# Masked attention: the row of maxima is transposed and spread two slots later, behind the fourth block of scores

## The chip, the core and the metric

The kernel runs on one core of a Trainium2 chip. The metric is the device time of one launch in microseconds (us); the time given is the median over runs. TensorE is called PE here, VectorE DVE, ScalarE ACT, GpSimd POOL, and SyncE, which issues the DMAs, SP.

## The reference, cut to what matters

Four layers, each added to its input: a masked attention, a modulated attention, and two recurrences over 256 steps. The change is in the first one. Its input x is 8 batches of 256 x 512 in float32; queries, keys and values are one and the same projection:

```python
q = xt @ Wq.T
qh = q.reshape(B, T, NH, dk).transpose(0, 2, 1, 3)      # 8 heads of 32
scores = scale * jnp.einsum('bhqd,bhkd->bhqk', qh, qh)
logits = (scores * cmask + (1.0 - cmask) * NEG) * rmask
attn = jax.nn.softmax(logits, axis=-1)
ctx = jnp.einsum('bhqk,bhkd->bhqd', attn, qh)
out = ctx @ Wo.T                                        # x = x + transposed out
```

Softmax is a quotient of sums of exponentials, so any number that is taken off all scores of one query cancels; it only keeps the exponentials in range. The kernel takes the query's largest score.

## The kernel before

Both attentions run interleaved in one loop over slots, `for g in range(-5, ...)`, U = 8 slots to a batch of the masked attention. A batch has two halves e of four heads each, and each half has four blocks kc of 128 keys. Within a slot the program is written out by hand: every engine gets its instructions in the order of the calls in the loop's body. `at(g, rel, n)` says which batch and which step r stand at slot g: it takes g - rel as 8 b + r.

A half passes through these steps:

- `scores0` (L205), slot 8b - 4 + 4e + kc: PE makes the scores of one block for four heads in four PSUM banks (s, L211), ACT copies them to a tile sc of 128 x 2048 (L216).
- `maxima0` (L219), same slot: DVE reduces sc to one maximum for each head and each row of the block, into a column of mxp0[e] (L221). The scores are symmetric, so rows of keys are as good as rows of queries. In the slots of blocks 0 to 2 it is called in the middle of the slot, in that of block 3 near its end.
- `rows0` (L225), once for each half: PE turns mxp0[e] into rows (pm, four transposes, L229), ACT copies them to mrow (L231), SP writes four rows, 8 KB, to DRAM (row, L234), and, when that has landed, reads them back for all 128 partitions (bc, 1 MB, L235). mrow and bc have one buffer each. So a new bc has to wait until the last block of the half before has used the old one.
- `weights0` (L237), slot 8b + 1 + 4e + kc: DVE takes bc off sc (L239). `exps0` (L241): ACT makes the exponentials (L243).
- `values0` (L245), slot 8b + 2 + 4e + kc: PE sums values and exponentials (pc, L254). `weigh0` (L262), after the fourth block: DVE's reciprocals (r, L271) and products, POOL's mask (ctxT, L273 and L274).
- `masked_out` (L276): the output projection (pso, L281), added to x by DVE (L284).

Before, rows0 stands at `at(g, -5, U)` with r = 3 or 7, that is in slots 8b - 2 and 8b + 2: in the slot of the third block of scores. At that place in the slot, the maxima of blocks 0 and 1 of this half have been called for; the columns of blocks 2 and 3 still hold what an earlier batch left there. Only the very first half (slot -1) has its rows made behind its own fourth block, by a call of its own.

The second attention fills the same slots: `qkv` (psqkv, L321), `maxima1` (n, L372, and its reduction L380), `rows1` (L382, with a copy mrow1 on ACT, L387), `weights1` (L389 to L411), `values1` (pc, L167), `modulated_out` (psx, L425). Its turned result is stored for later by `modulated_turn` (x2d, L448) on the same SP queue as row and bc, and so are the loads of x and mask for a batch to come (L78, L80). All score tiles, transposes and projections of both share one pool of five PSUM banks, handed out in turn. In slots whose number is 4 to 7 modulo 8, from 20 on, a1 is set (up to slot 63), and scores0 and rows0 are called behind the second attention's maxima1 and values1.

Of the kernel before, what the change touches and what calls it, by code (L numbers as in the profile page):

```python
# [24 lines left out]
def attention(ctx, tc, cst, x, cond, wqT, woT, w_emb, b_emb, g_norm, w_qkv, g_q, g_k, w_out, follow):  # L25
# [21 lines left out]
    U = 8  # L47
# [157 lines left out]
    def scores0(b, e, kc):  # L205

        qm = qms[b]
        ss = [bank([P, D], f"s0_{b}_{e}_{kc}_{h}") for h in range(4)]
        for h in range(4):
            r = 32 * h  # L210
            nc.tensor.matmul(  # L211
                ss[h], lhsT=qm[r : r + 32, e, kc * P : (kc + 1) * P], rhs=qm[r : r + 32, e, :], start=True, stop=True
            )
        sc = ftwo.tile([P, 4, D], F32, tag="sc", name=f"sc_{b}_{e}_{kc}", bufs=7)
        for h in range(4):
            nc.scalar.copy(sc[:, h, :], ss[h])  # L216
        scs[b, e, kc] = sc
# [7 lines left out]
    def rows0(b, e):  # L225

        pt = bank([P, NJ, P], f"pm0_{b}_{e}")
        for qc in range(NJ):
            nc.tensor.transpose(pt[:, qc, :], mxp0[e][:, qc, :], ident)  # L229
        mrow = ftwo.tile([P, D], F32, tag="mrow", name=f"mrow0_{b}_{e}", bufs=1)  # L230
        nc.scalar.copy(mrow, pt.rearrange("p q n -> p (q n)"))  # L231
        bc = bcs[b, e] = ftwo.tile([P, 4, D], F32, tag="bc", name=f"bc_{b}_{e}", bufs=1)
        row = dram.tile([4, D], F32, tag="row", name=f"row_{b}_{e}", bufs=2)
        nc.sync.dma_start(row, mrow.rearrange("(h i) n -> h i n", i=32)[:, 0, :])  # L234
        nc.sync.dma_start(bc, row.rearrange("h n -> (h n)").partition_broadcast(P).rearrange("p (h n) -> p h n", h=4))  # L235

    def weights0(b, e, kc):  # L237
        sc = scs[b, e, kc]
        nc.vector.tensor_sub(sc, sc, bcs[b, e])  # L239
# [22 lines left out]
    def weigh0(b, e):  # L262

        fill = ftwo.tile([P, D], F32, tag="fill", name=f"fill_{b}_{e}", bufs=1)
        nc.gpsimd.tensor_scalar(fill, mks[b], -1.0, means[b, e], ALU.add, ALU.mult)
        cx = ctxTs[b][:, e, :]
        pv, pn = pc0s[b, e]
        for i in range(2):
            t = slice(256 * i, 256 * i + 256)
            r = sm.tile([P, 256], F32, tag="r", name=f"r_0_{b}_{e}_{i}", bufs=2)  # L270
            nc.vector.reciprocal(r, pn[:, t])  # L271
            nc.vector.scalar_tensor_tensor(cx[:, t], r, 1e30, pv[:, t], ALU.min, ALU.mult)
        nc.gpsimd.tensor_tensor(cx, cx, mks[b], ALU.mult)  # L273
        nc.gpsimd.tensor_tensor(cx, cx, fill, ALU.add)  # L274
# [87 lines left out]
    def maxima1(b, c):  # L362
        qT, kT = qTs[b], kTs[b]

        ss = []
        for h in range(4):
            n = f"n1_{b}_{c}_{h}"
            ss.append(other_bank([P, 2, 256], f"c{h}", n) if b == B - 1 and h < 2 else bank([P, 2, 256], n))
        for qc in range(2):
            for h in range(4):  # L370
                r = 32 * h
                nc.tensor.matmul(  # L372
                    ss[h][:, qc, :],
                    lhsT=qT[r : r + 32, c, qc * P : (qc + 1) * P],
                    rhs=kT[r : r + 32, c, :],
                    start=True,
                    stop=True,
                )
        for h in range(4):
            nc.vector.tensor_reduce(mxp1[:, :, 32 * h], ss[h], AX.X, ALU.max)  # L380
# [32 lines left out]
    def values1(b, c):  # L413
        if c == 0:
            oTs[b] = big.tile([P, NJ, 256], F32, tag="oT", name=f"oT_{b}")
        pc = other_bank([P, 2, 256], "c2", f"pc1_{b}_{c}")
        for half in range(2):
            values(pc, half, lambda k, h: vts[b][:, k, c * P + h * DH : c * P + (h + 1) * DH], [exs1[b, c]])
        weigh(pc, oTs[b][:, c, :], f"1_{b}_{c}")
# [44 lines left out]
    def at(g, rel, n=1):  # L464

        b, r = divmod(g - rel, U)
        return (b, r) if 0 <= b < B and r < n else None

    def heads(g, rel, which=range(B)):

        for b in which:
            if 0 <= g - HEADS[b] - rel < NJ:
                return b, g - HEADS[b] - rel
        return None
# [3 lines left out]
    def leave(kind):  # L478
        for key in [k for k in left if k[0] == kind]:
            yield *key[1:], left.pop(key)  # L480

    with tc.manual_schedule():
        for g in range(-5, OUT[-1][1] + 2):

            a0, v0 = at(g, -4, U), at(g, 2, U)
            w1, v1 = heads(g, 1), heads(g, 2)

            a1, early = heads(g, 1, range(B - 2)), heads(g, 0, range(B - 2, B))
            late = a1 is not None or heads(g, 0, range(B - 2)) is not None
            turns = list(leave("qkv"))  # L490
            if a1:
                maxima1(*a1)
                if v1:
                    values1(*v1)
                if a := due.pop("weigh", None):
                    weigh0(*a)
            elif a0:
                scores0(a0[0], a0[1] // 4, a0[1] % 4)
            if (a := at(g, -5, U)) and a[1] % 4 == 3 and g > 0 and not a1:
                rows0(a[0], a[1] // 4)  # L500
            if v0 and not late:
                values0(v0[0], v0[1] // 4, v0[1] % 4)
            for a in leave("qt"):
                project_out(*a)
            if g == OUT[-1][1] + 1:
                cst["soon"]()
            for a in leave("x2"):
                modulated_turn(*a)
            if g - 1 in norms:
                modulate(norms.index(g - 1))  # L510
            if a1 and a0:
                scores0(a0[0], a0[1] // 4, a0[1] % 4)
            if (a := at(g, -5, U)) and a[1] % 4 == 3 and a1:
                rows0(a[0], a[1] // 4)
            if w1:
                rows1(*w1)
            if e0 := at(g, 1, U):
                weights0(e0[0], e0[1] // 4, e0[1] % 4)
                if not late:
                    exps0(e0[0], e0[1] // 4, e0[1] % 4)  # L520
            if v0 and not late and v0[1] % 4 == 3:
                weigh0(v0[0], v0[1] // 4)
            if a0 and a0[1] % 4 < 3:
                maxima0(a0[0], a0[1] // 4, a0[1] % 4)

            if a := at(g, -5, 2):
                left["qt", a[0], a[1]] = project(*a)
            if a := at(g, U + 2):
                masked_out(a[0])
            if 3 <= g < 7:  # L530
                modulation(2 * g - 6)
            if g == U:
                add_identity()
            if g in norms:
                normalize(norms.index(g))
            made = [(part, qkv(*part)) for part in parts.get(g, ())]
            for b in range(B):
                if g in OUT[b]:
                    m = OUT[b].index(g)
                    left["x2", b, m] = modulated_out(b, m)  # L540
            if a0 and a0[1] % 4 == 3:
                maxima0(a0[0], a0[1] // 4, 3)
            if g == -1:
                rows0(0, 0)
            for part, lines in made:
                if lines:
                    qkv_norm(*part, *lines)
                    left["qkv", *part] = lines[1]
            if not w1:
                for a in turns:  # L550
                    qkv_out(*a)
            if early:
                maxima1(*early)

            if v1 and not a1:
                values1(*v1)
            if w1:
                weights1(*w1)
                for a in turns:
                    qkv_out(*a)  # L560
            if e0 and late:
                exps0(e0[0], e0[1] // 4, e0[1] % 4)
            if v0 and late:
                values0(v0[0], v0[1] // 4, v0[1] % 4)
                if v0[1] % 4 == 3:
                    due["weigh"] = v0[0], v0[1] // 4
            if (a2 := at(g, -7)) and a2[0] > 1:
                load(a2[0])
            if g == -1:
                load_weights()  # L570
            if g == U * B + 2:
                first.close()
                follow()
                for (b, m), d in x2d.items():
                    nc.sync.dma_start(
                        cst["x2T"][:, :, b, m * P : (m + 1) * P], d.rearrange("p (j n) -> p j n", j=NJ)
                    )
# [486 lines left out]
```

## Time and profile before

| what | us |
|---|---|
| median of 3 runs | 2914.75 |
| lowest and highest | 2910.18, 2915.89 |
| the profiled execution, whole | 2913.32 |
| its span in the trace | 2910.6 |
| the two attentions, start to about | 836 |
| DVE: subtraction of bc (L239), one | 2.28 |
| DVE: maxima of a block (L221), one | 2.28 |
| ACT: copy to mrow (L231), one | 0.63 |
| PE: one transpose of maxima (L229) | 0.27 |

The span is the time between the first and the last instruction of one execution, and the rest of the execution lies around it. The chain that ended last is followed back from the last instruction: at each step to what released it, or to the instruction before it on its engine. "Waits" lists who stood idle for whom. In the chain and in waits, a name like `pm` is the tile that is written, with the number of the batch left out; `L229` is the line in the code above. PEld is PE's load of the stationary operand, which overlaps its matmuls. PEclk is the granted clock of PE, as a share of full speed.

### The profile page before, as it was taken

To read this page: it belongs to the slowest core of one execution; us is meant where nothing else is said; L and a number is where in the kernel's file an instruction comes from. 1 tells how busy PE (TensorE), PEld (TensorE's weight loads), DVE (VectorE), ACT (ScalarE), POOL (GpSimd) and SP (SyncE) were. 2 spreads that over 40 slices of the span, in tenths; PEclk is the share of its full clock that TensorE was granted. 3 is DMA by queue.
4 is the path that set the end of the run, shared out by engine and by line. 5 is a ranking of instruction groups with operands and counts; after the bars stand their busy time and mean duration, and the time that the engine had idled before them with its cause. 6 is when DMAs were issued, how large, how long until landed. Compare 5 with 4: busy or idle time off the path is not lost.

```text
span 2910.6 us, 159805 instructions
## 1 busy us (share of the span) xinstructions
PE 2705.6 (93%) x67258; PEld 1918.5 (66%) x67258; DVE 2126.1 (73%) x8951; ACT 1718.5 (59%) x8427; POOL 1098.7 (38%) x2945
## 2 busy tenths in 40 slices
PE   7799999999989999999999999999999999999996
PEld 3234444444557777777777777777777777777775
DVE  6767777676357777777777777777777777777774
ACT  5666566654346666666666666666666666666552
POOL 1144333443213444444444344444444434444442
PEclk8899999999999999999999999999999999999999
DMA  3111010101600000000000000000000000000000
GB/s 146 40 41 48 27 45 27 48 16 37 131 2 5 6 7 7 6 7 7 7 6 6 7 6 6 7 6 6 7 7 6 6 7 7 6 7 6 7 6 7
DMA packets 27558, 57.58 MB, mean 20 GB/s; under 512 B 2816, under 2 KB 17164, under 8 KB 24788
## 3 DMA queue, kind: packets, MB, share of 16 engines
q1 hardware_dynamic: 26836, 47.36, 5.5%
q8 instruction: 525, 8.60, 1.2%
q14 instruction: 197, 1.61, 0.2%
HBM read 40.15 MB, written 7.21 MB: 16 GB/s over the span
## 4 chain that ended last, share of the span: by engine, by line
PE 57%; DVE 29%; ACT 8%; issue 4%; POOL 1%; DMA 1%; ACTq 0%; SPq 0%; POOLq 0%; DVEq 0%
PE pg L795 19%; PE ic L760 18%; DVE icT L952 5%; PE psqkv L321 5%; DVE qn L953 5%; ACT tT L660 4%; DVE hqs L913 3%; PE pc L254 3%; DVE own L810 3%; DVE sqmm L909 2%; DVE v L812 2%; PE pc L167 2%; DVE hz L840 2%; PE s L211 2%; PE n L372 1%
## 5 line engine op out<-in xcount | busy, mean ns | idle before, releaser
L760 PE MATMUL ic<-cT_sb,tT 128*8 128x128 f32 x32736 | 1087.3, 273 | 82.4 <-ACT tT L660 44.6
L760 PEld LDWEIGHTS ic<-cT_sb,tT 128*8 128x8 f32 x32736 | 761.5, 89 | 340.1 <-ACT tT L660 271.6
L795 PE MATMUL pg<-whh_sb,hz 128*32 128x128 f32 x24576 | 819.0, 274 | 49.8 <-DVE hz L840 16.8
L660 ACT ACTIVATE tT<-qn 128x16 f32<-128x16 f32 x2046 | 439.8, 216 | 641.8 <-DVE qn L953 514.2
L795 PEld LDWEIGHTS pg<-whh_sb,hz 128*32 128x32 f32 x24576 | 667.8, 110 | 124.4 <-DVE hz L840 123.9
L952 DVE STREAM_TRANSPOSE icT<-ic 128x64 f32<-128x64 f32 x2048 | 504.2, 246 | 69.7 <-PE ic L760 64.7
L953 DVE SCALAR_TENSOR_TENSOR qn<-icT,hqs 128x16 f32<-128x16 f32 x2048 | 350.7, 171 | 70.1
L755 POOL TENSOR_TENSOR W<-W,cx 128x128 f32<-128x128 f32 x765 | 297.3, 389 | 256.1 <-ACT cx L741 256.0
L748 POOL TENSOR_TENSOR W<-cx,us 128x128 f32<-128x128 f32 x255 | 116.9, 458 | 446.4 <-ACT cx L741 446.4
L909 DVE SCALAR_TENSOR_TENSOR sqmm<-sqmm,qn 128x32 f32<-128x32 f32 x768 | 153.5, 200 | 151.5 <-ACT sqmm L898 122.9
L913 DVE TENSOR_TENSOR hqs<-W,sqmm 128x32 f32<-128x32 f32 x1020 | 199.9, 196 | 46.5 <-DVE own L835 1.1
L774 PE MATMUL gi<-wih_sb,x3T 128*32 128x384 f32 (+2 forms) x3072 | 202.4, 379 | 0.5 <-POOL x3T L965 0.5
L741 ACT ACTIVATE cx<-qn 128x32 f32<-128x32 f32 x1280 | 200.9, 213 | 0.2
L321 PE MATMUL psqkv<-wqkv_sb,xnT 128*128 128x512 f32 x384 | 174.6, 600 | 2.2 <-ACT sc L216 1.7
L221 DVE TENSOR_REDUCE mxp<-sc 128x4 f32<-128x2048 f32 x64 | 145.9, 2282 | 39.9 <-ACT sc L216 39.9
L741 ACT ACTIVATE cx<-p 128x32 f32<-128x32 f32 x1020 | 149.8, 217 | 32.3 <-DVE p L908 1.6
L216 ACT COPY sc<-s 128x512 f32<-128x512 f32 x256 | 131.5, 610 | 49.9 <-PE s L211 49.8
L810 DVE STREAM_TRANSPOSE own<-pg 128x128 f32<-128x128 f32 x256 | 84.8, 331 | 91.8 <-PE pg L795 91.8
L239 DVE TENSOR_TENSOR sc<-sc,bc 128x2048 f32<-128x2048 f32 x64 | 147.4, 2304 | 4.9 <-DMA bc<-row 4.8
L741 ACT ACTIVATE cx<-q 128x32 f32<-128x32 f32 x1020 | 145.5, 213 | 0.0
L243 ACT ACTIVATE sc<-sc,negT 128x2048 f32<-128x2048 f32 x64 | 129.1, 2019 | 20.2 <-DVE sc L239 20.2
L898 ACT ACTIVATE sqmm<-qn 128x32 f32<-128x32 f32 x768 | 140.4, 183 | 0.4
(149 smaller groups left out, 3353.8 us busy)
## 6 DMA issues: line engine op xcount, KB each, us to landing
bc<-row SPq DMA_DIRECT2D x16, 1024.0 KB
x<-in_x SPq DMA_DIRECT2D x8, 512.0 KB
out<-o SPq DMA_DIRECT2D x256, 16.0 KB
wqkv_sb<-in_L_cond_W_qkv SPq DMA_DIRECT2D x1, 3072.0 KB
wih_sb<-in_L_cond_W_ih SPq DMA_DIRECT2D x4, 768.0 KB
whh_sb<-in_L_cond_W_hh SPq DMA_DIRECT2D x4, 768.0 KB
x2d<-x2o SPq DMA_DIRECT2D x11, 256.0 KB
x2T<-x2d SPq DMA_DIRECT2D x11, 256.0 KB
```

The costliest lines, as they stand in the source:

```text
L321: nc.tensor.matmul(ps, lhsT=xnTs[b][:, c, m * P : (m + 1) * P], rhs=wqkv_sb[:, c, part * D : (part + 1) * D], start=(c == 0), stop=(c == N ...
L660: nc.scalar.activation(tT, src[:, half * HM : (half + 1) * HM, :], AF.Tanh)
L741: nc.scalar.activation(c[:, i], x, AF.Copy, scale=f)
L755: nc.gpsimd.tensor_tensor(W[:, i + 1 : 5], W[:, i + 1 : 5], c, ALU.add)
L760: nc.tensor.matmul(ps[32 * j : 32 * j + B, :], lhsT=tT[k // HM][:, k % HM, :], rhs=cT_sb[:, k, j * P : (j + 1) * P], start=(k == 0), stop= ...
L774: nc.tensor.matmul(gi_ps[rows(j), g0:g1, :], lhsT=x3T[c][:, k, :], rhs=wih_sb[:, k, g0:g1, j * P : (j + 1) * P], start=(k == 0), stop=(k = ...
L795: nc.tensor.matmul(pg_ps[rows(j), :], lhsT=hzs[tau % 3][:, k, 32 * g : 32 * g + 32], rhs=whh_sb[:, k, g, j * P : (j + 1) * P], start=((k, ...
L810: nc.vector.transpose(pgt.rearrange("p m n -> p (m n)"), pg_ps)
L909: stt(mm, sq, LIN[s], qs, ALU.subtract, ALU.mult)
L913: nc.vector.tensor_sub(hq, W[:, s], mm)
L952: nc.vector.transpose(icT.rearrange("p m n -> p (m n)"), ic[:, half * 64 : half * 64 + 64])
L953: stt(qn[:, m2, :], icT[:, :, 0:B], IC[s], hq[:, m2, :], ALU.mult, ALU.add)
```

## The change

rows0 is called two slots later: in slots 8b and 8b + 4, where the first block of the next half has its scores. All four blocks' maxima have been called for by then. Its place within the slot is the same, behind scores0. The half's first subtraction of bc, in slot 8b + 1 + 4e, stays where it was, so one slot lies between the two where there were three. The first half of all (slot -1) is unchanged.

```diff
-            if (a := at(g, -5, U)) and a[1] % 4 == 3 and g > 0 and not a1:
+            if (a := at(g, -3, U)) and a[1] % 4 == 3 and g > 0 and not a1:
                 rows0(a[0], a[1] // 4)
...
-            if (a := at(g, -5, U)) and a[1] % 4 == 3 and a1:
+            if (a := at(g, -3, U)) and a[1] % 4 == 3 and a1:
                 rows0(a[0], a[1] // 4)
```

## The prediction

> **What bounds the kernel now.** I read the page's slices first: TensorE (PE) is 9 tenths busy nearly everywhere, so only the attention stage (0 to about 836 us), which the change touches, can move. Then the chain that ended last, in order of time, because a sum over engines doesn't tell which wait is paid for. "Slot g" is one pass of the loop over g.
>
> Early slots, from the chain (start us, length us, engine, tile, line):
>
> ```profile
> 38.65 0.90 PE pm L229 x3
> 39.56 3.22 PE pc L254 x16
> ...
> 54.35 4.56 DMA bc<-row
> ...
> 67.73 0.90 PE pm L229 x3
> 68.62 3.57 PE pc L254 x16
> 72.20 3.51 PE pe L144 x16
> 75.71 2.06 PE s L211 x8
> ...
> 84.35 5.51 DMA bc<-row
> ...
> 98.67 0.90 PE pm L229 x3
> 99.57 3.57 PE pc L254 x16
> 103.14 3.94 PE pso L281 x8
> ```
>
> Five times before 165 us the chain runs through the transposes of the maxima (pm, L229): slots 2, 6, 10, 14, 18. Slots 2, 6, 10 are above. PE stands there in program order, with all that follows behind it:
>
> ```profile
> PE pm L229 <- DVE mxp L221: 20.3, 7, 9.0
> ```
>
> This is PE's largest wait between 20 and 180 us (us in total, times, longest). And the stretches (busy us per engine, then PEclk) show what a long wait does afterwards:
>
> ```profile
> 58.00:68.00 10.00, 6.17 (x50) 3.40 (x48) 9.00 (x8) 6.59 (x10) 3.16 (x4) 0.91 0.01 4
> 68.00:78.00 10.00, 10.00 (x47) 5.03 (x50) 6.73 (x7) 2.84 (x3) 2.77 (x2) 0.50 0.00 1
> ```
>
> At clock 0.50 the value matmuls (pc, L254) take 3.57 us; at 1.00 they take 1.85 (chain, from 110 us on).
>
> Steady slots (20 to 60, a period of 93.35 us for 8 slots, from row issues at 403.63 and 496.98): the transposes are on the chain in slots 26, 34, 42, 50, 58 alone, without a wait:
>
> ```profile
> 444.67 0.66 PE L229 MATMUL pm<-ident,mxp 128*128 128x128 f32 x4
> ```
>
> In slots 22, 30, 38, ... they aren't. There DVE runs without a gap from 398.07 to 415.5 us, and the chain's next scores wait for its maxima (L380).
>
> **The change part by part.** Counts stay: 15 of the 16 calls of rows0 move two slots later, each with 4 transposes, one copy on ACT (mrow, 0.59 to 0.63 us), a row DMA and a 1 MB bc DMA. DVE's and POOL's own orders are the same. On SP two x2d stores of each middle batch now stand ahead of the second head half's row and bc DMAs instead of behind them: they go out up to 24 us earlier, but between 260 and 700 us no instruction waits for an x2d store, so 0. The load of x behind bc in slots 9, 17, ... is issued as much later as bc is; its buffer is used 7 slots on, so 0.
>
> *1. What the early slots lose.* I follow each engine's order with the trace's own durations.
> Slot 2: pc need not stand behind pm; its exponentials end at 38.49, so it starts near 38.6 instead of 39.5: 0.9 gained.
> Slot 4: pm comes here. The last maxima end near 51.2, PE is free at 50.2: 1.0 wait plus 0.6. Row issue near 52.6, bc at 54.4 (1.75 later, as the chain has it for the first row), so the first subtraction (L239) of slot 5 is at 58.96 against 58.93: gain back to 0.
> Slot 6: pm would have waited 3.17 us behind maxima that stand behind two reciprocals on DVE. Without it pc starts at 64.7, not 68.6, and warm: 1.85 + 1.85 for pc and pe against 3.57 + 3.51. DVE's last maxima of slot 7 then end near 77.8 instead of 82.1: 4.3 gained.
> Slot 8: ACT's copies of the scores start at 77.5, mrow at 79.5, row at 80.15, bc at 81.9 instead of 84.35. Landing 5.5 (as there, with an x load behind it): 87.4 against 89.88, 2.5 left.
> Slots 10 and 11: the wait of 9.0 us goes; pso is ready by its data near 96.6 (103.1 before): 5.5 to 6.
> Slot 12: mrow follows copies at 113.0 to 115.0; bc 117.45, landing 4.5, so slot 13's subtraction is at 122.0 against 124.66: 2.65 left.
> Slots 14 to 16: the 1.38 wait and pm go; PE is 5.3 ahead at slot 16.
> Slot 16: copies at 142.2, bc 146.6 (150.0 before), landing 4.5 to 5.5: 151.1 to 152.1 against 154.43; the reciprocals behind it are 3.5 to 4.5 ahead, having waited for PE 1.1 before.
> Slot 18: 0.5 wait and 0.6 of pm go, and pso follows ctxT at 160.5 to 161.5 instead of 166.8: 5.3 to 6.3.
> I take 6.0 gained by slot 20.
>
> *2. Steady, removed.* Slot 42 and its like: pc starts 0.59 us after pm (444.67 to 445.26), and PE is then full to the end of psqkv (454.6), which the POOL chain of slot 43 hangs on. 5 x 0.59 = 2.95 gained. Slots 22 to 54 of the other kind: 0, since DVE is full.
>
> *3. Steady, added.* Slots 40: PE waits 1.15 us for ACT between scores and values:
>
> ```profile
> 424.00 2.07 ACT L216 COPY sc<-s 128x512 f32<-128x512 f32 x4
> 424.19 1.07 PE L254 MATMUL pc<-sc,qtok 128*32 128x512 f32 x8 [1.15 <-ACT sc L243]
> ...
> 434.24 2.28 DVE L239 TENSOR_TENSOR sc<-sc,bc 128x2048 f32<-128x2048 f32 x1
> ```
>
> 0.6 of pm fits into that; the mrow copy delays an exponential that ACT follows with 1.8 idle. Without that cover each would cost 0.6. Slots 36: 0.6 on PE ahead of the score matmuls, but the next matmuls (n, L372) take 1.97 instead of 1.15, waiting for ACT's exponentials: 0.8 of cover. Slot 60 has no scores; there mrow goes ahead of mrow1 on ACT, and L404 at once waits for that: 0.7 lost.
>
> *4. The new wait: bc.* Before, bc was issued when its buffer came free. Now it comes after copies, mrow, row: 1.91 + 0.66 + 1.75 = 4.3 us after the copies' start. Slot 40: 424.00 + 4.3 = 428.3; needed at 434.24, so there are 5.9 us for landing. Slot 36: 376.92 to 389.40 leaves 8.2. The trace has three landings that somebody waited for: 4.38, 4.56, 5.51; the others are shorter than their cover and show no length. Between 4.4 and 5.5 nothing waits. Queued behind that subtraction would be all of DVE's slot, and ACT's exponentials.
>
> Here the Trainium skill speaks against the change: "DMA: Bandwidth & Descriptors", section Bandwidth (Measured), gives 6.15 us for a 1 MB load without issue, by another queue. With its 0.6 to first byte (Latency and other measured facts), an estimate of 6.75: 0.85 lost in each of slots 24, 32, 40, 48, 56 = 4.2, and 4 x 1.75 = 7 in the early slots (4, 8, 12, 16; 5.0 assumed above on average), so the sum would be +3. The trace's own three, of the same transfer (8 KB read over and over), decide: I keep 4.5 to 5.5.
>
> The second rule is "TensorE: Matmul & The Clock Gate", section HAM oscillation: a PE gap over about 3.4 us halves the clock. The trace shows it after waits of 3.05, 3.17 and 9.0 us already (0.50 above). If the half clock stayed in slots 6 and 7 although the wait goes, 3.4 of gain would be late there; but DVE and bc, not PE, set slot 9, so it would take 1 or less from the sum. In slot 10 the gap shrinks to some 6.6, still cold, and I counted it so.
>
> *Sum:* -6.0 - 2.95 + 0.7 = -8.25, about -8. The profiled execution took 2913.32 (span 2910.6 and 2.7 around it), the median of the runs is 2914.75, 1.4 above: -8 from the median is 2906.8. Bounds: early part -3 (bc landings long, half clock) to -11 (every slot as slot 18); steady +1 to -4.
>
> **The rivals.**
> (a) Smaller: bc takes back most of the early gain, or DVE holds the steady slots. For: bc was waited for three times already. Gain -5.8 to 0, centre -4: 2911.
> (b) Slower: the bc round trip becomes the bound of half of the slots. Price per us of landing L: 5 x (L - 5.9) + 4 x (L - 5.0); it eats the 8 us at L near 6.3 and costs on from there. With L = 8 it is 10.5 + 12 - 8 = +14.5: 2929. Against: 5.51 is the longest seen. For: only three were seen; the wait for row reached 2.9 once where 1.3 is usual.
> (c) Larger: early waits pass on more than I let them, -12 to -16: 2901.
> (d) It doesn't do what it says: the transposes stay where they were. The order of instructions excludes it: on PE they stand behind the next half's first scores, on ACT the mrow copy stands behind those scores' copies.
>
> **How the numbers follow.** Main case 0.57 (-6 to -11), (a) 0.25, (b) 0.10, (c) 0.08. 0.2% is 5.8 us, about what a measurement of this kernel tells from no change. Faster: the main case but for its low end, and (c), 0.62; same 0.27: (a) and that low end; slower 0.11: (b) and 0.01 for mishaps that none of these names. The range leaves out (b)'s far part and half of (c): 2900 to 2914.
>
> **What would show it.** Right: PE's wait for mxp at L229 falls from 20.3 to below 5 us; the waits for bc stay at three or four, in slots 5, 9, 13, 17, not in 25, 33, 41; PEclk in 68 to 78 us rises; row issue to bc issue stays near 1.8; bc issue no longer lies at the end of a subtraction. Each x2d store of slot 42 goes out right after its copy, not after the bc DMA of two slots later. Wrong: DVE L239 waiting for bc in the steady slots, over 4 us in all, or a steady period of 93.35 or more instead of 92.8.

## The result and the profile after

| | median us | lowest | highest | runs |
|---|---|---|---|---|
| before | 2915.43 | 2910.18 | 2919.32 | 20 |
| after | 2908.76 | 2904.23 | 2914.97 | 20 |

The ratio is 0.998 (95% interval 0.9973 to 0.9988): 3.5 to 7.9 us less, 6.7 by the medians. Forecast were 8 less, 2906.8 us. As for the two traces: after's profiled execution is one of its slower ones (2913.18 us, span 2911.3), before's one of its quicker ones (2913.32, span 2910.6). In these two the attentions end at the same time (the first L760, a matmul of the recurrences behind them, at 835.90 and 835.86 us). So the traces show which waits changed; the gain itself is in the medians only.

The waits of PE between 20 and 180 us, after (us in total, times, longest):

```profile
PE pc L254 <- DVE ctxT L272: 8.9, 1, 8.9
PE pc L254 <- ACT sc L243: 4.8, 4, 3.3
...
PE pm L229 <- DVE mxp L221: 2.3, 2, 1.8
```

The transposes' wait fell from 20.3 us in 7 to 2.3 in 2, as foretold. But a line has come that before did not have: the value matmuls wait 8.9 us, once, for `ctxT`. It is in slot 10, where the longest wait (9.0) had stood. PE's timeline of after (start, length, in brackets the idle time ahead and its releaser):

```profile
99.85 1.93 PE L254 MATMUL pc<-sc,qtok 128*32 128x512 f32 x8 [8.86 <-DVE ctxT L272]
```

`values0` of a new half writes the same two PSUM tiles (c0 and c1, one buffer each) that `weigh0` of the half before reads. Before, PE stood at the transposes for maxima that follow that read on DVE, and the second wait lay hidden under the first:

```profile
89.88 2.29 DVE L239 TENSOR_TENSOR sc<-sc,bc 128x2048 f32<-128x2048 f32 x1 [2.56 <-DMA bc<-row]
...
98.67 0.90 PE L229 MATMUL pm<-ident,mxp 128*128 128x128 f32 x3 [9.01 <-DVE mxp L221]
```

The chain of after, early slots:

```profile
52.36 1.25 PE pm L229 x4
53.61 3.57 PE pc L254 x16
...
69.60 3.64 PE pc L254 x16
73.25 3.52 PE pe L144 x16
...
88.69 4.46 DMA bc<-row
...
93.17 2.29 DVE sc L239
...
99.85 3.38 PE pc L254 x16
103.23 3.63 PE pso L281 x8
```

Set beside before's: `pc` of slot 6 at 69.60 (68.62 before), `bc` of slot 8 issued at 88.69 (84.35 before), `pso` of slot 10 at 103.23 (103.14). From the first subtraction of slot 9 to that `pso` it is 10.1 us now and was 13.3 before: there the transposes' 3 us have gone. But the subtraction itself starts 3.3 later, and so `pso` gains nothing. `pm` now lies in slot 4 (52.36). The stretches (busy us per engine, then PEclk):

```profile
50.00:58.00 8.00, 8.00 (x39) 3.35 (x39) 6.76 (x4) 2.57 (x6) 0.21 (x1) 0.60 0.10 36
58.00:68.00 10.00, 10.00 (x74) 6.27 (x72) 6.37 (x6) 7.55 (x10) 0.88 (x2) 0.98 0.20 79
68.00:78.00 10.00, 8.79 (x44) 4.70 (x40) 9.65 (x11) 4.22 (x6) 5.15 (x3) 0.54 0.00 0
```

PEclk in 68 to 78 is 0.54, hardly above before's 0.50 (in a second trace of this kernel, below, it is 0.83). In 50 to 58 it is 0.60 although the profile shows PE busy for all 8.00 us of it; before had 1.00 there.

The page's row of the subtraction, after (busy, mean ns, then idle before and its releaser):

```profile
L239 DVE TENSOR_TENSOR sc<-sc,bc 128x2048 f32<-128x2048 f32 x64 | 148.5, 2321 | 9.6 <-DMA bc<-row 9.5
```

Before, it waited 4.8 us for `bc` in all. The 9.5 are 0.40 in slot 1, 4.47 in slot 9, 3.28 in slot 13, 0.90 in slot 17, and this in slot 41 (DVE's timeline):

```profile
435.05 2.88 DVE L239 TENSOR_TENSOR sc<-sc,bc 128x2048 f32<-128x2048 f32 x1 [0.44 <-DMA bc<-row]
```

In the steady slots the transposes have left the chain at slot 42, as foretold. These are neighbours in it from `pc` to `pso`, with no `pm` ahead:

```profile
446.13 1.85 PE pc L254 x16
...
448.58 3.44 PE pso L281 x8
```

By the starts of `pso` (L281) the steady period is 92.69 us where nothing disturbs it, against 93.35 in every period of before from slot 26 on. (The one from slot 18 to 26 is 94.77, and 94.09 before; below, "steady" leaves it out.) But the period that ends in slot 42 is 93.81: it holds the late `bc` of slot 40, which landed 6.44 us after its issue.

### The profile page after: what moved, and what is told of

Read it like the earlier page. It is cut to its first block, busy times and chain, and to the rows that moved or that the text cites. A ratio compares the mean times of both kernels' runs of the same rounds, so it can differ in the third digit from the quotient of the medians.

```text
span 2911.3 us, 159789 instructions
## 1 busy us (share of the span) xinstructions
PE 2711.6 (93%) x67258; PEld 1922.8 (66%) x67258; DVE 2127.1 (73%) x8951; ACT 1719.3 (59%) x8427; POOL 1096.2 (38%) x2945
## 4 chain that ended last, share of the span: by engine, by line
PE 57%; DVE 28%; ACT 8%; issue 4%; POOL 1%; DMA 1%; ACTq 0%; SPq 0%; POOLq 0%; DVEq 0%
PE pg L795 20%; PE ic L760 18%; DVE icT L952 5%; DVE qn L953 5%; PE psqkv L321 5%; ACT tT L660 4%; DVE hqs L913 3%; PE pc L254 3%; DVE own L810 3%; DVE sqmm L909 2%; DVE v L812 2%; PE pc L167 2%; PE s L211 2%; DVE hz L840 2%; PE n L372 1%
## 5 line engine op out<-in xcount | busy, mean ns | idle before, releaser
L760 PE MATMUL ic<-cT_sb,tT 128*8 128x128 f32 x32736 | 1086.5, 273 | 81.3 <-ACT tT L660 44.5
L760 PEld LDWEIGHTS ic<-cT_sb,tT 128*8 128x8 f32 x32736 | 760.0, 89 | 338.5 <-ACT tT L660 267.9
L239 DVE TENSOR_TENSOR sc<-sc,bc 128x2048 f32<-128x2048 f32 x64 | 148.5, 2321 | 9.6 <-DMA bc<-row 9.5
```

Of the source, the lines that this page charges most:

```text
L760: nc.tensor.matmul(ps[32 * j : 32 * j + B, :], lhsT=tT[k // HM][:, k % HM, :], rhs=cT_sb[:, k, j * P : (j + 1) * P], start=(k == 0), stop= ...
```

## The experiments

Each is set against runs of before on the same chip; a ratio of 0.998 is about 6 us less.

**The two halves of the change.** A helper picks the step; halves are counted from the first of all as 0.

```diff
+    def row_step(g):
+        for rel in (-3, -5):
+            a = at(g, rel, U)
+            if a and a[1] % 4 == 3 and (2 * a[0] + a[1] // 4 < 5) == (rel == -3):
+                return a
...
-            if (a := at(g, -3, U)) and a[1] % 4 == 3 and g > 0 and not a1:
+            if (a := row_step(g)) and g > 0 and not a1:
...
-            if (a := at(g, -3, U)) and a[1] % 4 == 3 and a1:
+            if (a := row_step(g)) and a1:
```

> Rows of the first four halves after the first (slots 4, 8, 12, 16) are made late as in the changed kernel, all later halves as before. The prediction's steps give this part nearly all of the 6 us less minus the 1 of slot 18: 5 less. Rival A: in slots 6, 10, 14 the value matmuls have to wait for the reciprocal products of the half before anyway (same two PSUM tiles), so the wait at the transposes was covered for all but one reduction of 2.2 us, and the bc chain takes that back: 0 to 2.5 less. Rival B: bc waits in slots 5, 9, 13, 17 cost more than the transposes gave: 1 to 4 more.

Measured: 2910.94 against 2912.42, ratio 0.9989 [0.998, 0.9998]: 3.2 us less, where the prediction's early term is 6.0. Its steady periods are 93.35 throughout, as before.

The same helper with `>= 5` moves the later rows alone:

> The reverse: the first four halves as before, all later ones late. The prediction's steps: 5 x 0.59 from slots 26 to 58, 1.1 from slot 18, minus 0.7 in slot 60: 3.3 less, with a steady period of 92.7 instead of 93.35. Rival A (early part gives little): this part is the larger one, 3 to 5 less. Rival C: steady slots are held by DVE, all comes from the early part: within 1 of before.

Measured: 2915.21, ratio 1.0005 [0.9995, 1.0014]: no gain. From slot 18 to 58 the periods of its trace are 92.24, 92.69, 95.44, 92.73, 92.69. In the longer one the `bc` of slot 40 landed 6.23 us after its issue, and that period gives back 2.1 of the 3.8 us that the other four save. So the step is real, and a `bc` that comes late once pays more than half of it out again. Why the median has no gain at all the trace doesn't show: its attentions end 5.5 us ahead of before's (the recurrences' first such matmul is at 830.31), and the recurrences, in which nothing was changed, then take 4.1 longer. From that matmul to the end the twelve traces take 2073.6 to 2078.9 us.

**The wait at the transposes by itself.** Rows stay where they were before, but the transposes of slots 2, 6, 10, 14 and 18 read a constant tile, so this kernel leaves out the maxima of these halves.

```diff
-            nc.tensor.transpose(pt[:, qc, :], mxp0[e][:, qc, :], ident)
+            nc.tensor.transpose(pt[:, qc, :], ones if 0 < 2 * b + e < 6 else mxp0[e][:, qc, :], ident)
```

> The kernel before, but the transposes of slots 2, 6, 10, 14, 18 read a constant tile instead of the maxima, so they stand in the same place and wait for nothing on DVE (the masked attention's numbers of these halves differ). bc is issued as early as before. The prediction's steps (nothing else holds the value matmuls): pc of slot 6 4.4 earlier, of slot 10 5.3, sum 9 to 13 less. Rival A (pc waits for the reciprocal products as well): 3.0 in slot 6, 3.0 in slot 10, sum 5 to 8 less, and PE's wait shows up at pc L254 behind DVE ctxT. Rival B' (DVE holds these slots): under 2 less.

Measured: 2906.04, ratio 0.9977 [0.9969, 0.9986]: 6.7 less, inside the rival's 5 to 8 and under the 9 to 13 that the prediction's steps would give. `pso` of slot 10 starts at 96.4 us. PE's timeline in slot 10:

```profile
92.83 1.93 PE L254 MATMUL pc<-sc,qtok 128*32 128x512 f32 x8 [6.54 <-DVE ctxT L272]
```

Of the 9.0 us of the transposes' wait, 6.5 stay when nothing but that wait is taken: the cover is shown. It gains 3.5 us more than the early part alone (6.7 against 3.2), and its `bc` is not later than before (slot 8: issued at 80.65): that fits a price of the later `bc` in the early slots, though the two intervals overlap (4.1 to 9.0 and 0.6 to 5.8).

**The changed kernel again**, with no edit, beside the three above:

> The changed kernel once more, for a second profile beside the others on the same chip. All theories: 0.2 to 0.3% less than before. If the early slots vary with the clock that PE happens to be granted, the time at which pso of slot 10 starts differs by 2 us or more from the first profile's 103.2 while steady periods agree within 0.2; if not, it agrees within 0.5.

Measured: 2910.13, ratio 0.9985 [0.9975, 0.9995]. `pso` of slot 10 starts at 101.08 us, 2.1 earlier than in the first trace of the same kernel. The periods from slot 18 on are 93.29, 92.69, 92.69, 97.56, 92.75. The long one, from its chain:

```profile
518.49 7.64 DMA bc<-row
526.15 2.32 DVE sc L239
...
535.56 2.07 PE s L211 x2
537.63 3.57 PE pc L254 x16
```

`bc` takes 7.64 us to land and DVE stands 1.67 us for it. The score and value matmuls that follow run at half speed (`pc` 3.57 instead of 1.85; PEclk 0.53 in 535 to 540), and the period is 4.9 longer than the quiet one.

**Is the tail of `bc` the load of x behind it?** The load is called one slot later.

```diff
-            if (a2 := at(g, -7)) and a2[0] > 1:
+            if (a2 := at(g, -6)) and a2[0] > 1:
```

> The changed kernel, with the loads of x and mask for a later batch issued one slot later (slots 10, 18, 26, 34, 42, 50 instead of 9, 17, ...), so that no x load runs right behind a bc. In the traces of the changed kernel one bc of slots 40 or 48 lands after 6.2 to 7.7 us where 5.9 are covered, in each execution. Theory: the x load behind it is what stretches it; then every steady period is 92.7, no subtraction of slots 25 to 57 waits for bc, and the time is 1 to 5 below the changed kernel's. Rival 1: a bc is late now and then by itself (a slow DMA engine, an instruction fetch): one bc in slots 20 to 60 still lands after 6 us and the time is within 1.5 of the changed kernel's. Rival 2: the x load, now in front of its first use, makes the projection of slot 43 wait: slower by 1 or more.

Measured: 2911.59 against 2913.26, ratio 0.9984 [0.9974, 0.9994], as the changed kernel. The landings of slots 40 and 48 are 7.37 and 6.32 us with no load near. The theory of the load fell.

The packets in the traces show another neighbour. A DMA queue that the page calls "instruction" moves packets of 16 KB, one at a time, at much the same places of the program in every trace. One of them falls on the late `bc` of the repeated kernel (packets, MB and share of that queue from 518 to 528 us):

```profile
q8 instruction: 1, 0.02, 0.9%
```

It starts at 518.57, and `bc` was issued at 518.49.

In the twelve traces, those of the runs below included, nine `bc` land more than 6 us after their issue: eight in slots 40 and 48, one in slot 8. In all nine such a packet starts within 0.2 us of the issue. In five more it does so too and `bc` lands within 6 us; without it no `bc` takes as long. Before, the packets of slots 40 and 48 went out at 428.51 and 522.50, when `bc`, issued at 423.12 and 516.46, had already landed; the change has moved its issue onto them. That this packet holds up a part of `bc` is the likely cause. No run here moves it alone, so it is not shown.

**Would the reciprocals in front of the subtraction use the wait for `bc`?** In the slots before 20, `weigh0` is called ahead of `weights0`.

```diff
+            first_weigh = g < 20 and v0 and not late and v0[1] % 4 == 3
+            if first_weigh:
+                weigh0(v0[0], v0[1] // 4)
             if e0 := at(g, 1, U):
                 weights0(e0[0], e0[1] // 4, e0[1] % 4)
```

> The changed kernel, with weigh0 (reciprocals and products of the half before) ahead of the subtraction of bc on DVE in slots 5, 9, 13, 17. Theory: in the early slots the wait for bc costs because the reciprocals stand behind it on DVE, and the value matmuls of slots 6, 10, 14 wait for those products (PE pc L254 behind DVE ctxT, 8.9 in one trace). Then that wait falls below 4, pso of slot 10 starts 3 to 5 earlier, and the time is 4 to 8 below the changed kernel's. Rival: DVE is full in these slots, the order within it doesn't matter, and the subtraction that now stands behind 4.2 us of reciprocals holds the exponentials instead: within 1.5 of the changed kernel's, or slower.

Measured: 2922.75, ratio 1.0027 [1.0016, 1.0039]: slower than before, and `pso` of slot 10 starts at 105.03 us, not earlier. PE's waits from 20 to 180 us say why:

```profile
PE pc L254 <- ACT sc L243: 21.2, 5, 7.6
```

The reciprocals wait for PE's last `pc` themselves, and the subtraction, which the exponentials and the next `pc` hang on, now stands behind both. In the chain of slot 9 the subtraction starts at 97.17, after reciprocals from 92.83 to 96.72.

The same with the later load, and in slot 60 `rows1` ahead of `rows0`:

```diff
-            if (a := at(g, -3, U)) and a[1] % 4 == 3 and a1:
+            if (a := at(g, -3, U)) and a[1] % 4 == 3 and a1 and a0:
                 rows0(a[0], a[1] // 4)
             if w1:
                 rows1(*w1)
+            if (a := at(g, -3, U)) and a[1] % 4 == 3 and a1 and not a0:
+                rows0(a[0], a[1] // 4)
```

> Both edits of the two other kernels, and in slot 60 the second attention's row of maxima ahead of the masked one on PE and ACT. If both theories hold: 6 to 13 below the changed kernel's, the fastest of all; slot 60 alone 0.7. If only the reciprocals' place matters: 4 to 8; if neither: within 1.5.

Measured: 2920.34, ratio 1.0021 [1.0013, 1.0029]. Waits for `bc` are down to 0.7 us in all and every steady period is 92.69, and yet it is slower than before: what the order on DVE costs in the early slots outweighs both. Slot 60 can't be told from this run.

**How much a longer landing costs.** Each `bc` DMA is made twice.

```diff
         nc.sync.dma_start(bc, row.rearrange("h n -> (h n)").partition_broadcast(P).rearrange("p (h n) -> p h n", h=4))
+        nc.sync.dma_start(bc, row.rearrange("h n -> (h n)").partition_broadcast(P).rearrange("p (h n) -> p h n", h=4))
```

> The changed kernel with each bc transfer made twice in a row to the same place, to see the cover that the prediction gave: 5.9 us in slots 24 to 56 of the first halves, 8.2 in those of the second halves, 5.0 in the four early slots. If the second transfer waits for the first, landing is 9 to 10 us: 5 x 3.6 + 5 x 1.3 + 4 x 4.5 = some 43 more than the changed kernel. If they run back to back, 7.4: 5 x 1.5 + 0 + 4 x 2.4 = some 17 more. Rival (bc hidden by other waits of DVE's slot): under 6 more.

Measured, in two runs: 2938.31, ratio 1.0085 [1.0062, 1.0107], some 29 us above the changed kernel (24.8 over its before, where the changed kernel is 4 to 5 under). DVE's waits over the whole span (the added line makes L239 L240):

```profile
DVE sc L240 <- DMA bc<-row: 62.5, 16, 9.6
```

A landing is about 9.0 us now. In the steady slots the waits are what the prediction's cover says: about 3.0 (9.0 less 5.9) in slots 25 and 33, and 1.1 (9.0 less 8.2) in slots 21, 29 and 37. Two periods are only 0.45 and 0.6 us longer than the quiet 92.69: what DVE waits in them is nearly all made up. The two with slots 40 and 48, where landings took 11.7 and 10.5 us, are 5.1 and 2.3 longer. The early slots pay in full: waits of 5.65, 5.99, 8.44, 9.63 and 5.92 in slots 1, 5, 9, 13 and 17, and `pso` of slot 18 starts at 190.31 us, not at 166 to 167.

**One slot instead of two.** The runs above suggest that late transposes are good and a late `bc` is bad, so I tried the place between: rows behind the scores of the fourth block.

```diff
-            if (a := at(g, -3, U)) and a[1] % 4 == 3 and g > 0 and not a1:
+            if (a := at(g, -4, U)) and a[1] % 4 == 3 and g > 0 and not a1:
...
-            if (a := at(g, -3, U)) and a[1] % 4 == 3 and a1:
+            if (a := at(g, -4, U)) and a[1] % 4 == 3 and a1:
```

> The changed kernel, but with the rows called one slot later than before, not two (slots 8b - 1 and 8b + 3, where the fourth block's scores are made; the fourth block's column is then still the earlier batch's, as the third's and fourth's were before). bc is again issued when its buffer comes free, at the end of a subtraction one slot ahead, so it has some 9 us or more to land instead of 5.9. If the steady gain is the place of the transposes alone (away from the slots of weigh0's wait) and what eats it is the bc that lands late, the steady period is 92.69 in every batch with no longer one, no subtraction from slot 20 on waits for bc, and the time is 2904 to 2909 (6 to 11 below before). Rival: the transposes are on the chain in the slots of the fourth block as well; then the period is 93.35 as before, and only what the early slots give is left: 2910 to 2914. Second rival: the longer periods have nothing to do with bc's cover; then one of them is still 1 to 5 us over 92.69, with bc early.

Measured, in five runs: 2900.31 (2898.36 to 2905.27) against 2911.53, ratio 0.9961 [0.9948, 0.9973]: 8 to 15 us less than before, the best of all, and under its own forecast. Its steady periods are 93.15 to 93.17, none longer. `bc` has 11.0 to 11.6 us to land (8.2 in the last half), and from slot 20 on nobody waits for it. By their packets these landings end 3.8 to 5.3 us after the issue, so the longer cover was not called on: `bc` goes out at 418.69 and 511.85 us, well ahead of the instruction packets of slots 40 and 48 (424.29 and 517.46). The page's row of the subtraction:

```profile
L239 DVE TENSOR_TENSOR sc<-sc,bc 128x2048 f32<-128x2048 f32 x64 | 147.7, 2307 | 4.1 <-DMA bc<-row 4.1
```

Both guesses at the period missed (92.69 and 93.35): the transposes do lie on the chain in slot 39, but cost less than the 0.66 that two slots save:

```profile
409.93 0.59 PE pm L229 x4
410.74 3.44 PE psqkv L321 x8
```

In slots 8 to 10 the chain shows the gain, against 84.35, 89.88 and 103.14 before, and 88.69, 93.17 and 103.23 in the changed kernel:

```profile
81.47 6.42 DMA bc<-row
87.91 2.29 DVE sc L239
...
94.59 3.64 PE pc L254 x16
98.23 4.07 PE pso L281 x8
```

`bc` is issued when its buffer comes free, and that is 2.9 us earlier than before: slot 6 has no wait for maxima, its `pc` starts at 67.44 at full speed, and PEclk in 68 to 78 is 0.86, not 0.50.

The early rows two slots later and all others one:

> The rows of the first four halves after the very first two slots later (as changed), all later ones one slot later. If bc's cover is what matters in the steady slots, they run at 92.69 with no longer period, and with the early slots as in the changed kernel the time is 2906 to 2909. If the transposes lie on the chain in the fourth block's slot, the period is 93.35 and the time 2910 to 2913, as with the early part alone. Beside the kernel with all rows one slot later, it tells what the early slots prefer: earlier bc (that one is faster by 1 to 4) or transposes that wait for nothing (this one is).

Measured: 2904.51, ratio 0.9976 [0.9964, 0.9988]: 7.0 less. Periods 93.13 throughout. Beside the kernel above it is about 4 us slower, and 3.3 of these are there by `pso` of slot 18 (166.22 and 162.88): the early slots prefer the earlier `bc`. Beside the early part alone (ratio 0.9989, on another chip) it is better by some 4, but that is not shown to be the rows' doing. Its trace is 1.8 us ahead of the early part's at slot 66, and 3.2 more come behind it, where no rows are left. The same stretch in before and in the kernel with all rows one slot later:

```profile
789.04 5.29 PE L425 MATMUL psx<-wout_sb,oT 128*128 128x512 f32 x8
...
782.49 3.60 PE L425 MATMUL psx<-wout_sb,oT 128*128 128x512 f32 x8
```

Both stand behind the same wait of 1.97 us for maxima; PEclk is 0.66 in the first 5 us of the one and 1.00 in those of the other. Ten traces take 4.9 to 5.3 us here, the two with rows one slot later 3.6, and the second of these is 1.2 quicker in the next `pc` (L167) as well. So some 3 us of the gain of these two kernels is a higher clock behind the rows. Whether the move brings that clock with it is open.

## Why the prediction was right, and where its steps were not

The forecast of 8 less was right as a whole: 6.7, in a measured interval of 3.5 to 7.9. Its mechanism holds in the main: PE's wait at the transposes goes, that wait taken by itself is worth 6.7, and a later `bc` takes a part back. That the sum came so near is in part luck: moved alone, its two terms, -6.0 and -2.25, measured -3.2 and +1.5. And by slot 18 the traces with late early rows are at most 1.1 us ahead of before's: `pso` starts there at 165.7 to 167.1 us where DVE's order is kept, and at 166.8 before. By its own steps:

- **The wait at the transposes goes, and `bc` becomes the wait of slots 9, 13, 17: right.** 20.3 us fell to 2.3; waits for `bc` in those slots are 4.47, 3.28 and 0.90. Slot 5, also named, had none in this trace and 0.74 in the second one. Not all signs came as named: slot 41 waited for `bc` too (0.44), `bc` of slot 8 followed its row by 2.6 us and not by 1.8, and PEclk in 68 to 78 us rose clearly in the second trace only (0.83).
- **The cover of `bc`: right.** From issue to subtraction there are 5.90 us (first halves) and 8.24 (second halves), where 5.9 and 8.2 were forecast; the run with `bc` made twice shows its waits where these say.
- **Slot 4 "gain back to 0", slot 6 "`pc` starts at 64.7", slot 8 "bc at 81.9": failed.** I followed DVE and `bc` through slots 4 and 5, but PE has no idle time there after 43 us. `pm` (1.25 with its wait, at 52.36) and a half clock went onto it: slot 5's `pc` starts at 63.13 instead of 58.30 (60.66 in the second trace), the reciprocals behind it wait for PE, and slot 6's `pc` is at 69.60 (68.67), not earlier than before. In the first trace the half clock also stayed in slots 6 and 7. So the scores and rows of slot 8 came late, and `bc` was issued at 88.69 (86.22).
- **Slot 10 "5.5 to 6": failed, and by slot 8's `bc`.** `pso` was to be ready at 96.6; it started at 103.2 and 101.1. The forecast had counted the gap of "some 6.6" that stays, though it did not name `ctxT` as what ends it: where the wait alone was taken and `bc` stayed early, 6.54 us stayed and `pso` started at 96.4. In every kernel that keeps DVE's order, `pso` of slot 10 starts 10.0 to 10.3 us after the first subtraction of slot 9 where that wait is gone, and 13.2 after it where it stands. So 3.0 us are gained, and what `bc` is late comes off them.
- **The early term, -6.0:** mis-sized. Moved by itself it gave -3.2 (interval -5.8 to -0.6).
- **Steady, removed, 5 x 0.59:** right per period (0.66), but mis-sized in the sum. Rival (b), a `bc` beyond its cover, comes true in small: in five of the six profiled executions with these rows two slots late and one transfer each (all but the one with both edits), landings of 6.1 to 7.7 us in slot 40 or 48 made one or two periods 0.2 to 4.9 us longer. Moved by itself, the steady part gave +1.5 (interval -1.5 to +4.1). That the longest of three seen landings (5.51) was taken as the bound for the new time of issue is the step that failed. At the old time it was a fair one: by its packets every `bc` of before ends within 5.6 us of its issue. What the prediction put at nothing is that `bc`, issued at another time, meets other traffic.
- **Slot 60, +0.7:** not settled. From slot 58 to 66 four traces with late rows there (the changed kernel twice, the later part, the later load) take 88.7 to 90.3 us; before takes 89.5, and the early part alone, with the rows there where they were, 88.0.
- **Price of a longer landing:** 5 x (L - 5.9) + 4 x (L - 5.0) overrates the steady slots, which absorb most, and underrates the early ones: the run with L about 9.0 lost 23 us up to slot 18 and some 7 in the five periods after it (against the first trace of the changed kernel). Part of the 23 is the wait in slot 1, whose row the formula leaves out. Its break-even comes out at 6.4, not 6.3, and was not tested as such.

Against the Trainium skill, "DMA: Bandwidth & Descriptors", section Bandwidth (Measured): its 6.15 us for 1 MB with 0.6 to the first byte is not what `bc` usually takes (4.2 to 5.5 us where it was waited for), so the trace was the better guide to the middle. That the late landings of 6.1 to 7.7 lie around that estimate is no support for it: most of a late transfer runs as fast as the others, and only its tail is late.

What stays open: the two parts alone add to -1.7 with an uncertainty of about 4, the whole measured -6.7 and, again, -4.4. Noise can hold this, a joint effect too. Nor is it settled what the best kernel gains by its rows: of the 7.5 us between its span and before's, 3.9 are there by slot 18, 2.3 more come by slot 66, 3.6 by the first L760 (most of it the clock behind the rows), and 2.3 are lost after it. Untested is whether a `bc` issued away from the instruction packets would let the two-slot move keep its 92.69.

## What to carry to other kernels

A wait that goes uncovers the next one on the same engine: before counting it as gained, ask what the instruction behind it needs (here a PSUM tile with one buffer that another engine still reads). A transfer's length at one time of issue is no bound for another: moved, it meets other traffic, and with its cover cut to near its usual time one late `bc` (the period of 97.56) took back more than the other four periods of its execution had saved. Between "early data" and "late consumer" try the middle place: one slot was worth more than two here, in part by a clock that was higher where no rows are left. And follow a gain to the end of the trace, past the last place that was changed.

## What the hardware showed that I had not expected

- The same transfer of 1 MB, where it was waited for most often 4.2 to 5.5 us, took 6.1 to 7.7 in slots 40 or 48 (and 6.42 once in slot 8). In such a landing the rate per half microsecond falls from some 400 GB/s to 33 GB/s or less for the last stretch. Each of these has a 16 KB packet of the instruction queue within 0.2 us of its issue; that this is the cause is likely and not shown. The load of x is not the cause.
- PE ran at 0.60 in 50 to 58 us without any idle time that the profile shows in that stretch; before had 1.00 there. The prediction counted a wait of 3.05 us at 36 to 39 among those that halve the clock, but before's PEclk is 0.50 from 28 us on already, so that one shows nothing. In the changed kernel a wait of 1.21 us ahead of slot 6's `pc` goes with 0.54 in 68 to 78 us; in its second trace a wait of 1.10 at the same place goes with 0.83 and a `pc` at full speed. And in the repeated kernel a wait of PE of only 1.87 us (ahead of the scores at 535.56) was followed by 0.53 for 5 us; so 1.67 us of DVE's waiting became 4.9. The Trainium skill's gap of about 3.4 us ("TensorE: Matmul & The Clock Gate", HAM oscillation) is not the shortest that a slow clock goes with here.
- Instruction for instruction the same early slots end at different times: `pso` of slot 10 starts at 103.07 and 100.62 in the two kernels that have before's early rows, at 103.16 and 101.08 in the changed one. One pair of traces can't carry a difference of 2 us there.
